# FFN inputs of twelve passes: transposed in 32x32 blocks and copied between partitions instead of on the matmul engine

## The chip, the cores and the metric

The kernel runs on one core of a Trainium2 chip. A core has a matmul engine (TensorE, PE in the profile), a vector engine (VectorE, DVE), a scalar engine for activations and copies (ScalarE, ACT), a general one (GpSimd, POOL) and a sync engine (SyncE, SP) that issues transfers. They run side by side, each in the order of its own instructions, and wait for each other through semaphores. SBUF is the on-chip memory with 128 partitions; PSUM is where TensorE puts its results. The metric is the device time of one execution in microseconds (us).

## The reference

A batch of 2048 tokens x (512 values each) goes through two residual layers.

- First layer: the layer norm of x goes through one of four experts, chosen by the token's id. An expert has one matrix M (its transpose is `ctxT`), used for all three products: `y = (silu(h M^T) * (h M^T)) M^T`. Then `x = x + tanh(g_xattn) * y`.
- Second layer: the layer norm of the new x goes through a feed-forward network, `h = silu(silu(xr w1^T) w3^T) w2^T`, and a router picks the two largest of eight logits `xr wr^T` for each token. The gated rows are added up by expert number with `out.at[indices].add(...)`, so only the first eight rows of the flat output receive anything, the sums over all tokens. They are multiplied by `tanh(g_ffn)`.

Everything is 32-bit floating point.

## The kernel before

**Passes.** The tokens are sorted by expert and cut into 17 passes of 128 rows: 13 full passes (numbers 0 to 12, one expert each) and four shared ones (13 to 16), in which four groups of 32 rows have each their own expert. A full pass needs one 1 MB matrix, a shared pass four. `order` (line 383) says in which place each pass is worked: here the shared passes stand in places 6, 10, 13 and 16.

**A round.** The loop over `i` (line 876) works on several passes at once. Its program order, which is each engine's order (the schedule is written by hand), is:

- `up(order[i])`: TensorE computes z, ScalarE and VectorE make g from it (lines 466, 467);
- `turn_in(order[i+1])`: TensorE transposes the next pass's normalized input (tp_a), ScalarE copies it to SBUF as hT;
- `centre(order[i+2])`: VectorE's statistics and subtraction on the pass after that;
- `gather(order[i+3])` on GpSimd's queue and `load(order[i+3])` of its matrices on SyncE's queue, into seven buffers (`mp`);
- `down(order[i-1])`: TensorE computes y, VectorE adds it to x (line 481), GpSimd scatters the rows to the output;
- `turn_out(order[i-2])`: TensorE transposes the second norm's output h_f with four 128x128 transposes (tp_f, line 380), and ScalarE copies the result into hT2, the FFN's input (line 515; for a shared pass in four pieces at computed places, line 527);
- `norms(order[i+2], order[i-1])`: VectorE's statistics of the new x, two inverse roots of nine small operations each (lines 355 to 373), and h_f = (x - mean) * rs (line 505);
- a `step()` of the FFN, if a block runs;
- `turn_mid(order[i])`: TensorE transposes g (tp_g);
- another `step()`.

**The FFN.** It works on two blocks of 1024 tokens. `sums_of_hT` (line 591) starts a block: TensorE computes the router's logits for both halves (`lg`, tag x, a PSUM pool of two buffers), VectorE subtracts two quarters of the input (T1), turns the logits in 32x32 blocks (`lt`, line 710) and makes T2 to T4. `first_layer` computes the 2x2 block product with seven products (X, Y and Z; the T and S sums feed them), where X takes the tag x too. It yields after every second product, seven times for a block. `second_layer` computes v, four tiles for each half, one a step, and `acc` adds the gated rows up. A block has 15 steps (block 1 ends with some longer ones). Block 0 starts in the round of place 10, with no step at that round's end; block 1 starts when the last pass has been turned out.

**Queues.** SyncE issues the matrices, the weights (w1 and wr in the round of place 2, w3 and w2 in that of place 7) and the final rows, in program order, and waits for a buffer to come free before an issue. GpSimd issues gathers and scatters.

The line that lets block 0 start without a step, and the allocation of the logits:

```python
            if last[b] == i - 2:
                hT_sums[b] = sums_of_hT(b)
                running.append(ffn(b))
        if last[0] != i - 2:
            step()
...
        lg = ps_x.tile([P, P], F32, tag="x", name=f"lg_{b}_{half}")
...
            xs_[c] = ps_x.tile([P, HB], F32, tag="x", name=f"X_{b}_{c}")
```

Of the kernel before, what the change touches and what calls it, by code (L numbers as in the profile page):

```python
# [25 lines left out]
def tile_gated_moe_ffn(  # L26
# [39 lines left out]

    nc = tc.nc
# [17 lines left out]
    mp = ctx.enter_context(tc.tile_pool(name="mp", bufs=7))  # L85
    xp = ctx.enter_context(tc.tile_pool(name="xp", bufs=5))
# [26 lines left out]
    def load_w(src, name):  # L113
        w = ct_([P, KC, src.shape[1]], F32, name)
        nc.sync.dma_start(w, src.rearrange("(k p) f -> p k f", p=P))
        return w
# [188 lines left out]
    def row_tables():  # L305

        pad = ct_([P, NP], F32, "pad")
        nc.vector.tensor_scalar(pad, tok, 1.0, float(4 * NT), ALU.is_lt, ALU.mult)
        nc.vector.scalar_tensor_tensor(to_row, tok, -1.0, pad, ALU.add, ALU.add)

        pads = ct_([P, E], F32, "pads")
        nc.vector.tensor_sub(pads, size[:, 2, :], num[:, 0, :])
        behind = ct_([P, E, NU - NF], F32, "behind")
        nc.vector.tensor_tensor(
            behind,
            later[:, E : 2 * E, NF:NU],
            pads.unsqueeze(2).to_broadcast([P, E, NU - NF]),
            ALU.mult,
        )
        psum = ct_([P, NU - NF], F32, "psum")  # L320
        nc.vector.tensor_reduce(psum, behind.rearrange("p e n -> p n e"), AX.X, ALU.add)
        nc.vector.tensor_sub(psum, place0[:, NF:NU], psum)
        nc.vector.tensor_scalar(
            first, psum, float(-(NB - 1) * TB), float(TB), ALU.add, ALU.min
        )


    hT2 = [ct_([P, KC, TB + (Q if b == NB - 1 else 0)], F32, f"hT2_{b}") for b in range(NB)]
# [9 lines left out]
    def moments(xt, name):  # L338
        st = small.tile([P, 6], F32, tag="st", name=f"st_{name}")
        nc.vector.bn_stats(st, xt)  # L340
        mv = small.tile([P, 2], F32, tag="mv", name=f"mv_{name}")
        nc.vector.bn_aggr(mv, st)
        return mv

    def inverse_roots(mvs_, names):


        n = range(len(names))

        def new(tag):  # L350
            return [small.tile([P, 1], F32, tag=tag, name=f"{tag}_{name}") for name in names]

        v, r, q, w, rs = new("v"), new("r"), new("q"), new("w"), new("rs")
        for i in n:
            nc.vector.tensor_scalar_add(v[i], mvs_[i][:, 1:2], EPS)
        for i in n:
            nc.vector.tensor_scalar(
                r[i].bitcast(I32), v[i].bitcast(I32), -0.5, float(0x5F3759DF), ALU.mult, ALU.add
            )
        for i in n:  # L360
            nc.vector.scalar_tensor_tensor(q[i], r[i], v[i], r[i], ALU.mult, ALU.mult)
        for i in n:
            nc.vector.tensor_scalar(w[i], q[i], 0.375, -1.25, ALU.mult, ALU.add)
        for i in n:
            nc.vector.tensor_scalar(w[i], w[i], q[i], 1.875, ALU.mult, ALU.add)
        for i in n:
            nc.vector.tensor_mul(r[i], r[i], w[i])
        for i in n:
            nc.vector.scalar_tensor_tensor(q[i], r[i], v[i], r[i], ALU.mult, ALU.mult)
        for i in n:  # L370
            nc.vector.tensor_scalar(q[i], q[i], -0.5, 1.5, ALU.mult, ALU.add)
        for i in n:
            nc.vector.tensor_mul(rs[i], r[i], q[i])
        return rs
# [8 lines left out]
    order = [0, 1, 2, 3, 4, 5, NF, 6, 7, 8, NF + 1, 9, 10, NF + 2, 11, 12, NF + 3]  # L383
    assert sorted(order) == list(range(NP))
    xs, x1s, mvs, rss, hs, hTs, gTs, gs, hs2, mats = {}, {}, {}, {}, {}, {}, {}, {}, {}, {}

# [9 lines left out]

    def centre(p):

        mvs[p] = moments(xs[p], f"a{p}")
        hs[p] = work.tile([P, D], F32, tag="h", bufs=4, name=f"h_a{p}")  # L400
        nc.vector.tensor_scalar(hs[p], xs[p], mvs[p][:, 0:1], None, ALU.subtract)  # L401

    def scale(*ps):
        for p, rs in zip(ps, inverse_roots([mvs.pop(p) for p in ps], [f"a{p}" for p in ps])):
            rss[p] = rs
# [6 lines left out]
    def first_in(p):  # L412

        st = small.tile([P, 6], F32, tag="st", name=f"st_a{p}")
        nc.vector.bn_stats(st, xs[p])
        mvs[p] = small.tile([P, 2], F32, tag="mv", name=f"mv_a{p}")
        nc.vector.bn_aggr(mvs[p], st)
        hTs[p] = work.tile([P, KC * P], F32, tag="hT", bufs=2, name=f"hT_{p}")
        n = D // 2
        for i in range(2):  # L420
            h = work.tile([P, n], F32, tag="h", bufs=4, name=f"h_a{p}_{i}")
            nc.vector.tensor_scalar(
                h, xs[p][:, i * n : (i + 1) * n], mvs[p][:, 0:1], None, ALU.subtract
            )
            tp = ps_tp.tile([P, n], F32, tag="tp", name=f"tp_a{p}_{i}")
            for k in range(n // P):
                nc.tensor.transpose(tp[:, k * P : (k + 1) * P], h[:, k * P : (k + 1) * P], ident)
            nc.scalar.copy(hTs[p][:, i * n : (i + 1) * n], tp)  # L428

    def load(p):  # L430

        n0, n = (p, 1) if p < NF else (NF + (p - NF) * G, G)
        mats[p] = []
        for i in range(n0, n0 + n):
            at = nc.values_load(
                look_up(i),
                engines=[SP],
                min_val=0,
                max_val=(E - 1) * D,
                skip_runtime_bounds_check_because="an expert's number, times D",  # L440
            )
            m = mp.tile([P, KC, D], F32, tag="m", name=f"m_{i}")
            nc.sync.dma_start(m, ctxT[bass.ds(at, D), :].rearrange("(k p) f -> p k f", p=P))
            mats[p].append(m)
# [47 lines left out]
    def norms(p_in, p_out):  # L492


        if p_out is None:
            return
        xt = x1s.pop(p_out)
        mv = [moments(xt, f"f{p_out}")]
        names = [f"f{p_out}"]
        if p_in is not None:  # L500
            mv.append(mvs.pop(p_in))
            names.append(f"a{p_in}")
        rs = inverse_roots(mv, names)
        h = work.tile([P, D], F32, tag="h", bufs=4, name=f"h_f{p_out}")
        nc.vector.tensor_scalar(h, xt, mv[0][:, 0:1], rs[0], ALU.subtract, ALU.mult)
        hs2[p_out] = h
        if p_in is not None:
            rss[p_in] = rs[-1]

    def turn_out(p):  # L510

        tp = transposed(hs2.pop(p), f"f{p}").rearrange("p (k t) -> p k t", k=KC)
        if p < NF:
            b, t = divmod(p, TB // P)
            nc.scalar.copy(hT2[b][:, :, t * P : (t + 1) * P], tp)  # L515
            return
        for i in range(G):
            n = (p - NF) * G + i
            place = NF * P + n * Q - (NB - 1) * TB
# [3 lines left out]
                min_val=min(place - E * (Q - 1), TB),  # L523
                max_val=min(place, TB),
                skip_runtime_bounds_check_because="its place less at most E (Q - 1) pads, at most TB",
            )
            nc.scalar.copy(hT2[NB - 1][:, :, bass.ds(at, Q)], tp[:, :, i * Q : (i + 1) * Q])
# [47 lines left out]
    def sums_of_w1():  # L575

        h = D // 2
        a11, a12 = w1[:, 0:2, 0:h], w1[:, 2:4, 0:h]
        a21, a22 = w1[:, 0:2, h:D], w1[:, 2:4, h:D]
        ss = [ffp.tile([P, 2, h], F32, tag=f"S{i}", name=f"S{i}") for i in range(1, 5)]  # L580
# [10 lines left out]
    def sums_of_hT(b):  # L591
# [3 lines left out]
        b11, b12 = hT2[b][:, 0:2, 0:HB], hT2[b][:, 0:2, HB:TB]  # L595
        b21, b22 = hT2[b][:, 2:4, 0:HB], hT2[b][:, 2:4, HB:TB]
        ts = [ffp.tile([P, 2, HB], F32, tag=f"T{i}", name=f"T{i}_{b}") for i in range(1, 5)]
# [7 lines left out]
    def first_layer(b):  # L605
# [14 lines left out]
        def product(out_ps, a, bb, c, start):  # L620
            for k in range(2):
# [3 lines left out]
                    bb[:, k, :],  # L625
# [66 lines left out]
    def logits(b, half):  # L692
# [3 lines left out]
        for k in range(KC):  # L696
            cols = hT2[b][:, k, half * HB : (half + 1) * HB].rearrange("p (t c) -> p t c", t=TT)
# [127 lines left out]
    last = {b: max(i for i, p in enumerate(order) if min(p // (TB // P), NB - 1) == b) for b in range(NB)}  # L825
# [20 lines left out]
    load(order[0])  # L846
# [3 lines left out]
    load(order[1])  # L850
# [8 lines left out]
    load(order[2])  # L859
    nc.sync.dma_start(gates[:, 0:1], g_xattn.to_broadcast([P, 1]))  # L860
    nc.sync.dma_start(gates[:, 1:2], g_ffn.to_broadcast([P, 1]))
    load(order[3])
# [10 lines left out]
    load(order[4])  # L873
    summing = sums_of_w1()
    owed = []
    for i in range(2, NP + 2):
        if i < NP:
            up(order[i])
        if i + 1 < NP:
            turn_in(order[i + 1])  # L880
        if i + 2 < NP:
            centre(order[i + 2])
        if i + 3 < NP:
            gather(order[i + 3])
            load(order[i + 3])
        if i <= NP:
            down(order[i - 1])
        turn_out(order[i - 2])
        if i <= NP:
            norms(order[i + 2] if i + 2 < NP else None, order[i - 1])  # L890
        step()
        if i > NP:
            step()
        if 5 <= i < 9:
            next(summing)
        if i == 2:
            w1 = load_w(w1T, "w1")
            wr = load_w(wrT, "wr")
        if i == 7:
            w3 = load_w(w3T, "w3")  # L900
            w2 = load_w(w2T, "w2")
        if i < NP:
            turn_mid(order[i])
        for b in range(NB):
            if last[b] == i - 2:
                hT_sums[b] = sums_of_hT(b)
                running.append(ffn(b))
        if last[0] != i - 2:
# [54 lines left out]
```

## Time and profile before

| what | value |
|---|---|
| time, median of 3 runs | 279.15 us (279.06 to 279.7) |
| profiled execution | 277.53 us, its span 275.8 us |
| PE, DVE, ACT, POOL busy | 97%, 54%, 25%, 14% |
| granted TensorE clock | 1.0 throughout |
| tp_f transposes | 68, 17 passes of four |
| h_f on VectorE (line 505) | 17 of 542 ns |
| x after y on VectorE (line 481) | 17 of 749 ns |
| statistics of the new x (line 340) | 17 of 695 ns |
| transposes of the logits (line 710) | 4 of 303 ns |
| SyncE's issue of a matrix | 372 ns at the least, 2479 ns at the most |
| moved by DMA | 42.54 MB, mean 154 GB/s |

In a row of groups the columns are the line, the engine, the operation, its output and inputs by name, their shape and how many there are; after the bar the busy time in us and the mean of one in ns; after the second bar the idle time just before them and what ended it. A row of the order of time has the start in us, the duration in us, the engine, the line, the operation, its names and how many were merged; in brackets stands the idle time before it. Starts and ends of matmuls in the order of time are modelled and overlap by some tenths; the chain that ended last merges the same work without overlaps.

### The profile page before, as it was taken

The page shows a single profiled execution, that of the slowest core. Times are in us where ns is not written, and L with a number is a line of the kernel's source. Part 1 is how long each engine was busy: PE and PEld are TensorE (multiplying, and loading weights), DVE is VectorE, ACT ScalarE, POOL GpSimd, SP SyncE. Part 2 cuts the span into 40 slices and gives each one's busy share as a digit, 9 for nine tenths or more (in the row PEclk, how much of TensorE's full clock was granted, in tenths as well). Part 3 has the DMA queues.
Part 4 walks back from the last instruction along what each step waited for, and adds up shares of the span by engine and source line. Part 5 has one row for each costly group of instructions (what it writes and reads, how often), then busy time and mean ns, then how long its engine had stood idle before and what let it go on. Part 6 is the DMA issues. An engine that isn't in the chain of part 4 may idle for free.

```text
span 275.8 us, 3562 instructions
## 1 busy us (share of the span) xinstructions
PE 266.6 (97%) x1173; PEld 125.4 (45%) x1173; DVE 148.7 (54%) x593; ACT 69.3 (25%) x134; POOL 39.3 (14%) x63
## 2 busy tenths in 40 slices
PE   5889999999999999999999999999999999999994
PEld 2445455544355454444344444534245444344362
DVE  6677877777888769918263481516253620711000
ACT  2022232232232231223143232312113233311120
POOL 6520122221122211211110010101010000000000
PEclk9999999999999999999999999999999999999999
DMA  0697998545669996697304084001000000000000
GB/s 1 217 354 277 408 402 334 173 155 206 228 225 402 389 409 258 173 398 264 112 26 166 2 312 180 38 0 40 0 12 2 0 0 1 0 0 2 0 0 2
DMA packets 20722, 42.54 MB, mean 154 GB/s; under 512 B 2143, under 2 KB 2207, under 8 KB 20704
## 3 DMA queue, kind: packets, MB, share of 16 engines
q1 hardware_dynamic: 17952, 33.66, 34.0%
q0 software_dynamic: 2720, 8.65, 8.3%
q8 instruction: 9, 0.15, 0.2%
q14 instruction: 9, 0.07, 0.1%
q10 hardware_dynamic: 32, 0.01, 0.0%
HBM read 38.10 MB, written 4.47 MB: 154 GB/s over the span
## 4 chain that ended last, share of the span: by engine, by line
PE 94%; DVE 2%; DMA 2%; issue 1%; ACT 0%; DVEq 0%
PE z L453 22%; PE y L453 21%; PE v L730 20%; PE X L622 10%; PE Y L622 5%; PE tp_f L380 3%; PE tp_a L380 3%; PE tp_g L380 3%; PE Z L622 2%; PE acc L742 1%; PE lg L699 1%; DMA x<-in_x_dram,from_row 1%; DMA idt<-in_ids_dram 1%; PE accT L758 1%; PE o L814 0%
## 5 line engine op out<-in xcount | busy, mean ns | idle before, releaser
L453 PE MATMUL z<-m,hT 128*32 128x512 f32 (+1 forms) x232 | 61.8, 595 | 0.2 <-ACT hT L428 0.2
L453 PE MATMUL y<-m,gT 128*32 128x512 f32 (+1 forms) x232 | 61.4, 594 | 0.0
L730 PE MATMUL v<-w,s 128*128 128x512 f32 (+1 forms) x136 | 57.3, 570 | 0.0
L730 PEld LDWEIGHTS v<-w,s 128*128 128x128 f32 x136 | 25.0, 190 | 27.2 <-issue 26.7
L453 PEld LDWEIGHTS z<-m,hT 128*32 128x32 f32 (+1 forms) x232 | 22.6, 146 | 29.5 <-issue 28.1
L453 PEld LDWEIGHTS y<-m,gT 128*32 128x32 f32 (+1 forms) x232 | 22.6, 146 | 27.8 <-issue 27.8
L482 POOL DMA_INDIRECT out_dram<-x,to_row x17 | 17.2, 1011 | 84.9 <-DVE x L481 82.7
L389 POOL DMA_INDIRECT x<-in_x_dram,from_row x17 | 16.7, 984 | 77.5 <-DVE h_a L401 22.9
L467 DVE SCALAR_TENSOR_TENSOR g<-z,rs_a,g 128x512 f32<-128x512 f32 x17 | 12.7, 750 | 27.1 <-ACT g L466 27.0
L466 ACT ACTIVATE g<-z,rs_a 128x512 f32<-128x512 f32 x17 | 11.7, 687 | 51.3 <-PE z L453 51.3
L481 DVE SCALAR_TENSOR_TENSOR x<-y,tg,x 128x512 f32<-128x512 f32 x17 | 12.7, 749 | 16.9 <-PE y L453 16.8
L738 ACT ACTIVATE s<-v 128x512 f32<-128x512 f32 (+1 forms) x17 | 9.7, 572 | 41.9 <-PE v L730 41.9
L515 ACT COPY hT<-tp_f 128x512 f32<-128x512 f32 x13 | 7.6, 587 | 43.5 <-PE tp_f L380 43.5
L340 DVE BATCH_NORM_STATS2 st_a<-x 128x6 f32<-128x512 f32 x16 | 11.0, 688 | 7.5 <-DMA x<-in_x_dram,from_row 7.5
L622 PE MATMUL X<-T,S 128*128 128x512 f32 x32 | 15.0, 592 | 0.0
L380 PEld LDWEIGHTS tp_f<-ident,h_f 128*128 128x128 f32 x68 | 8.2, 141 | 10.2 <-issue 10.2
L340 DVE BATCH_NORM_STATS2 st_f<-x 128x6 f32<-128x512 f32 x17 | 11.8, 695 | 0.6
L380 PEld LDWEIGHTS tp_a<-ident,h_a 128*128 128x128 f32 x64 | 7.7, 140 | 9.4 <-issue 9.1
L640 DVE TENSOR_TENSOR s<-X,c 128x512 f32<-128x512 f32 x4 | 2.8, 692 | 16.2 <-PE X L622 16.2
L473 ACT COPY gT<-tp_g 128x512 f32<-128x512 f32 x17 | 10.0, 586 | 5.3 <-PE tp_g L380 5.3
L380 PE MATMUL tp_f<-ident,h_f 128*128 128x128 f32 x68 | 10.4, 276 | 0.0
L380 PE MATMUL tp_g<-ident,g 128*128 128x128 f32 x68 | 10.2, 273 | 0.0
(165 smaller groups left out, 271.6 us busy)
## 6 DMA issues: line engine op xcount, KB each, us to landing
m<-in_ctxT_dram SPq DMA_DIRECT2D x29, 1024.0 KB
w<-in_w1T_dram SPq DMA_DIRECT2D x1, 1024.0 KB
w<-in_w3T_dram SPq DMA_DIRECT2D x1, 1024.0 KB
w<-in_w2T_dram SPq DMA_DIRECT2D x1, 1024.0 KB
x<-in_x_dram,from_row POOLq DMA_INDIRECT x17, 6.2
out_dram<-x,to_row POOLq DMA_INDIRECT x17, 6.1
wr<-in_wrT_dram SPq DMA_DIRECT2D x1, 64.0 KB
x_first<-out_dram SPq DMA_DIRECT2D x4, 4.0 KB
```

The source lines that it names most:

```text
L340: nc.vector.bn_stats(st, xt)
L380: nc.tensor.transpose(tp[:, k * P : (k + 1) * P], h[:, k * P : (k + 1) * P], ident)
L389: nc.gpsimd.indirect_dma_start(out=xt, out_offset=None, in_=x, in_offset=bass.IndirectOffsetOnAxis(ap=from_row[:, p : p + 1], axis=0),)
L453: nc.tensor.matmul(out_ps[i * n : (i + 1) * n, :], lhs[:, k * P + i * n : k * P + (i + 1) * n], m[:, k, :], start=(k == 0), stop=(k == KC ...
L466: nc.scalar.activation(g, z, AF.Silu, scale=rs)
L467: nc.vector.scalar_tensor_tensor(g, z, rs, g, ALU.mult, ALU.mult)
L473: nc.scalar.copy(gT, tp)
L481: nc.vector.scalar_tensor_tensor(xt, y, tg[:, 0:1], xt, ALU.mult, ALU.add)
L482: nc.gpsimd.indirect_dma_start(out=out, out_offset=bass.IndirectOffsetOnAxis(ap=to_row[:, p : p + 1], axis=0), in_=xt, in_offset=None, bou ...
L622: nc.tensor.matmul(out_ps, a[:, k, c * P : (c + 1) * P], bb[:, k, :], start=start and k == 0, stop=k == 1, skip_group_check=True,)
L730: nc.tensor.matmul(v, s1[:, k, c_b + t * P : c_b + (t + 1) * P], w3[:, k, c0 : c0 + n], start=(k == 0), stop=(k == KC - 1),)
L738: nc.scalar.activation(s2, v, AF.Silu)
```

## The change

Passes 0 to 11 no longer go through TensorE for the FFN's input.

- `norms` computes for them only the inverse root and a shift (-mean * rs). Both roots, that of the pass going out and that of the pass coming in, are computed together as two columns in 11 operations. `norm_out`, two rounds after the pass's `up`, makes h_f on ScalarE with scale and shift.
- `turn_set` transposes h_f on VectorE in 32x32 blocks, which leaves the blocks in the wrong partitions. Four passes make a set. When a set is complete, `exchange` issues 16 copies on SyncE's queue, each from 32 partitions to 32 partitions within SBUF with 2 KB a partition, which put the blocks of the set's four passes in their places. The turned sets 0 and 1 lie in s1, which the FFN writes later, set 2 in the buffer that w2 takes afterwards.
- hT2 is four tiles of 512 tokens, each one half of a block: three of them are filled by exchanges, the last by `turn_out` as before (passes 12 to 16). The products and logits read a half as four pieces of 128 columns.
- The shared passes move to places 9, 12, 14 and 16.
- Matrices are loaded as soon as the seventh one before has been used (`load_free`), after `down`, instead of three places ahead. w1 and wr move to the round of place 3, w3 to that of place 12 and w2 to that of place 16. The sums of w1 (S) move from the rounds of places 5 to 8 to 6 to 9; the third of them is written over a quarter of w1.
- x gets six buffers instead of five, h three instead of four.
- The first `step()` of a round stands before `norms` instead of behind it. Block 0 starts in the round of place 11, and a step follows at once. The rounds of places 13 and 15 get a third step.

```diff
-    xp = ctx.enter_context(tc.tile_pool(name="xp", bufs=5))
+    xp = ctx.enter_context(tc.tile_pool(name="xp", bufs=6))
...
-    hT2 = [ct_([P, KC, TB + (Q if b == NB - 1 else 0)], F32, f"hT2_{b}") for b in range(NB)]
+    NS = NF // 4 * 4
+    hT2 = [ct_([P, G, KC, P], F32, f"hT2_{b}") for b in range(NB * 2 - 1)]
+    hT2.append(ct_([P, KC, HB + Q], F32, "hT2_last"))
...
+    def inverse_roots(var, name):
+        n = var.shape[1]
...
+        nc.vector.tensor_scalar_add(v, var, EPS)
+        nc.vector.tensor_scalar(
+            r.bitcast(I32), v.bitcast(I32), -0.5, float(0x5F3759DF), ALU.mult, ALU.add
+        )
+        square()
+        nc.vector.tensor_scalar(w, q, 0.375, -1.25, ALU.mult, ALU.add)
+        nc.vector.tensor_mul(w, w, q)
+        nc.vector.scalar_tensor_tensor(r, w, 1.875, r, ALU.add, ALU.mult)
+        square()
+        nc.vector.tensor_scalar(q, q, -0.5, 1.5, ALU.mult, ALU.add)
+        nc.vector.tensor_mul(rs, r, q)
...
-    order = [0, 1, 2, 3, 4, 5, NF, 6, 7, 8, NF + 1, 9, 10, NF + 2, 11, 12, NF + 3]
+    order = [0, 1, 2, 3, 4, 5, 6, 7, 8, NF, 9, 10, NF + 1, 11, NF + 2, 12, NF + 3]
...
+    def load_free(i):
+        n = len(loaded)
+        while n < len(units) and (n < MP or order.index(units[n - MP][0]) < i):
+            n += 1
+        load(n - len(loaded))
...
+        if p_out < NS:
+            shift = small.tile([P, 1], F32, tag="shift", name=f"shift_{p_out}")
+            nc.vector.scalar_tensor_tensor(
+                shift, mv[:, 0, 0:1], -1.0, rs[:, 0:1], ALU.mult, ALU.mult
+            )
+            scaled[p_out] = rs[:, 0:1], shift
+            return
...
+    def norm_out(p):
+        rs, shift = scaled.pop(p)
+        h = work.tile([P, D], F32, tag="h", bufs=3, name=f"h_f{p}")
+        nc.scalar.activation(h, x1s.pop(p), AF.Identity, bias=shift, scale=rs)
+        hs2[p] = h
...
+    def turn_set(p):
+        b, i = divmod(p, 4)
+        nc.vector.transpose(
+            turned_set(b).rearrange("p q (k i t) -> p k q i t", i=4, t=Q)[:, :, :, i, :],
+            hs2.pop(p).rearrange("p (k q t) -> p k q t", k=KC, q=4),
+        )
+
+    def exchange(b):
+        for q in range(4):
+            for g in range(G):
+                nc.sync.dma_start(
+                    hT2[b][q * Q : (q + 1) * Q, g].rearrange("p k c -> p (k c)"),
+                    turned_set(b)[g * Q : (g + 1) * Q, q, :],
+                )
...
+        if before_last < NS:
+            norm_out(before_last)
         if i + 2 < NP:
             centre(order[i + 2])
         if i + 3 < NP:
             gather(order[i + 3])
-            load(order[i + 3])
+        if before_last in (7, 11):
+            turn_set(before_last)
+        if before_last == 7:
+            exchange(1)
         if i <= NP:
             down(order[i - 1])
-        turn_out(order[i - 2])
+        load_free(i)
+        if before_last == 11:
+            exchange(2)
+        if before_last >= NS:
+            turn_out(before_last)
+        step()
         if i <= NP:
             norms(order[i + 2] if i + 2 < NP else None, order[i - 1])
-        step()
         if i > NP:
             step()
-        if 5 <= i < 9:
+        if 6 <= i < 10:
             next(summing)
-        if i == 2:
+        if i == 3:
             w1 = load_w(w1T, "w1")
             wr = load_w(wrT, "wr")
-        if i == 7:
+        if i == 12:
             w3 = load_w(w3T, "w3")
+        if i == 16:
             w2 = load_w(w2T, "w2")
         if i < NP:
             turn_mid(order[i])
-        for b in range(NB):
-            if last[b] == i - 2:
-                hT_sums[b] = sums_of_hT(b)
-                running.append(ffn(b))
-        if last[0] != i - 2:
+        if i == 11:
+            hT_sums[0] = sums_of_hT(0)
+            running.append(ffn(0))
+        if i == NP + 1:
+            hT_sums[1] = sums_of_hT(1)
+            running.append(ffn(1))
+        step()
+        if before_last in hs2:
+            turn_set(before_last)
+            if before_last == 3:
+                exchange(0)
+        if i in (13, 15):
             step()
```

## The prediction

> **What bounds the kernel now.** I read the engines' busy shares first, then the chain of work that ended last, then the groups by line, and last the order of time at the two places where the change alters what TensorE (PE) meets. All times are us.
>
> ```profile
> PE 266.6 (97%) x1173; PEld 125.4 (45%) x1173; DVE 148.7 (54%) x593; ACT 69.3 (25%) x134; POOL 39.3 (14%) x63
> ...
> PE 94%; DVE 2%; DMA 2%; issue 1%; ACT 0%; DVEq 0%
> PE z L453 22%; PE y L453 21%; PE v L730 20%; PE X L622 10%; PE Y L622 5%; PE tp_f L380 3%; PE tp_a L380 3%; PE tp_g L380 3%; PE Z L622 2%; PE acc L742 1%; PE lg L699 1%; DMA x<-in_x_dram,from_row 1%; DMA idt<-in_ids_dram 1%; PE accT L758 1%; PE o L814 0%
> ...
> L515 ACT COPY hT<-tp_f 128x512 f32<-128x512 f32 x13 | 7.6, 587 | 43.5 <-PE tp_f L380 43.5
> ...
> L380 PE MATMUL tp_f<-ident,h_f 128*128 128x128 f32 x68 | 10.4, 276 | 0.0
> ```
>
> PE is the bound from the first product to the last: the chain is 94% PE, and its pieces follow each other without a gap from 24 on. So every us that leaves PE leaves the time, unless PE has to wait where it did not. tp_f, the transposes of the FFN's inputs, is 3% of the chain. Its mean of 276 ns includes pipelining; the place it really takes is in the order of time.
>
> The order of time where FFN block 0 begins (pass in place 10):
>
> ```profile
> 101.34 0.60 PE L380 MATMUL tp_f<-ident,h_f 128*128 128x128 f32 x4
> 101.78 0.60 PE L380 MATMUL tp_g<-ident,g 128*128 128x128 f32 x4
> 101.79 0.74 DVE L481 SCALAR_TENSOR_TENSOR x<-y,tg,x 128x512 f32<-128x512 f32 x1
> 102.31 1.95 PE L699 MATMUL lg<-hT,wr 128*32 128x128 f32 x64
> 102.56 0.69 DVE L340 BATCH_NORM_STATS2 st_f<-x 128x6 f32<-128x512 f32 x1
> 104.19 3.70 PE L453 MATMUL z<-m,hT 128*128 128x512 f32 x8
> 105.43 0.54 DVE L505 TENSOR_SCALAR h_f<-x,mv_f,rs_f 128x512 f32<-128x512 f32 x1
> 105.89 1.22 DVE L598 TENSOR_TENSOR T<-hT 128x1024 f32<-128x1024 f32 x1
> 107.03 0.50 DVE L710 STREAM_TRANSPOSE lt<-lg 128x128 f32<-128x128 f32 x2
> ```
>
> Four tp_f take 0.44 of PE (101.34 to 101.78). VectorE (DVE) turns the router's logits (lt) only at 107.03, long after PE made them; PE has the next z to do meanwhile.
>
> And where block 1 begins:
>
> ```profile
> 207.24 0.60 PE L380 MATMUL tp_f<-ident,h_f 128*128 128x128 f32 x4
> 207.68 3.60 PE L730 MATMUL v<-w,s 128*128 128x512 f32 x8
> 209.22 0.27 ACT L527 COPY hT<-tp_f 128x128 f32 x1 [0.16 <-ACT hT L527]
> 209.52 1.23 DVE L598 TENSOR_TENSOR T<-hT 128x1024 f32<-128x1024 f32 x1 [5.32 <-ACT hT L527]
> 211.21 1.95 PE L699 MATMUL lg<-hT,wr 128*32 128x128 f32 x64
> 213.09 1.98 PE L622 MATMUL X<-hT,w 128*128 128x512 f32 x4
> ```
>
> Here one step of block 0 (v, 3.44 in the chain) covers ScalarE's (ACT) four copies, which end at 209.49, and T.
>
> **The change, part by part.**
>
> *Transposes gone from PE.* 12 of 17 passes lose four tp_f each: 12 x 0.435 (0.43 and 0.44 at 51.40 and 101.34) = 5.2 saved on the bound. Behind a shared pass's y the chain gives tp_f 0.59; three of the removed ones stand there, and I take it that the next transpose inherits the extra 0.16 (if not, 5.7).
>
> *Their place in the chain.* The ACT copy (587 ns) becomes an Identity with scale and bias; the SBUF-to-SBUF Silu of 629 ns and the one with a scale per row of 687 ns bound it. ACT is 25% busy and it comes behind the two ACT jobs that PE awaits: nothing. On DVE h_f (0.54) goes, 18 small operations of 1.92 together (45.19 to 47.11) become 11 dependent ones and a shift at 0.2 each, the pace of a lone chain (nine from 201.75 to 203.65): 2.4. A 32x32-block transpose of 128x512 comes in; the 128x128 one took 303 ns, a quarter of the elements. 512 columns cost bn_stats 695 ns and four single transposes would cost 1.21; I take 0.7, because other 128x512 operations with one result per input are all near it. DVE's round was 6.29 (stt x 0.77, st_f 0.73, aggregate 0.22, roots 1.92, h_f 0.55, stt g 0.75, st_a 0.72, aggregate 0.22, h_a 0.41); now it is 6.3 + 0.7 = 7.0, and 7.7 in four rounds with a sum of w1 (0.68). PE's round falls from 8.18 to 7.74. g is then ready 1.3 to 2.0 before its transposes: nothing.
>
> *48 copies on SP's queue.* SP spent 0.28 to 0.37 on an issue (L915, L443), so 16 take 4.5 to 6, and 1 MB moves in 2.6 at the 400 GB/s of the busy slices. I put the transpose of set 1 at 90.0 on the new clock, its copies landing by 98 to 100, and the logits that read it at 106.6: covered by 7 to 9. Behind it on SP stands one matrix, needed at 115. Set 0 has nearly 40 in hand, set 2 three rounds; behind set 2 stand only w2 and the small x_first loads.
>
> *Loads by free buffers.* SP waits for y of the seventh matrix before. Tightest are the last two matrices of the passes in places 14 and 16, issued as the shared y two rounds earlier ends. Before, three loads issued at 157.64 had moved two loads' worth by 166.0: 8.4. PE has 10.9 to do by then (three steps of 3.44, a transpose, 0.16): 2.5 in hand, nothing lost. w1 moves behind the matrix that waits for y of place 2 (about 43), and its sums start at 66; w3 is issued some 15 ahead of its use.
>
> *New wait 1, block 0's start.* Before, no step followed the logits of block 0. Now one does, in the round of place 11, and its first product X takes a PSUM buffer (two share the tag x) that the logits hold until DVE has turned them. DVE runs in program order: x, the statistics and roots of that round, T1, then lt. In the chain y ended at 101.51, and the first lt at 107.03 + 0.30 = 107.33: 5.8 later. PE gets from y to X in 0.44 + 0.44 + 1.88 = 2.75. The difference is 3.1; DVE's x will no longer be held 0.25 by h_a (59.75 to 59.78 where it wasn't), and the roots cost 0.1 to 0.2 more than what goes. I take 3.0, between 2.8 and 3.4. Queued behind X on PE is everything.
>
> *New wait 2, block 1's start.* Steps: block 0 has 15; they now begin one earlier and two are added at places 13 and 15, so all are spent a round before the end, where one was left before to stand at 207.68. tp_f ends at 207.84 in the chain; the copies end 1.65 later, T1 2.9, lt 3.25. Half 0's logits (0.94) no longer depend on those copies, half 1's end at 2.65. X starts at 3.25 where 1.88 would be ideal: 1.4, between 1.1 and 1.75 (both halves waiting).
>
> *Sum.* -5.2 + 3.0 + 1.4 = -0.8. The profiled execution took 277.53 (span 275.8 and 1.7 around it), 1.6 under the median of 279.15; I carry the difference over: 279.15 - 0.8 = 278.35.
>
> [...]
>
> **The rivals.**
>
> *Fewer new waits.* Speaking for it: I infer which buffer X takes. Without wait 2 the time is 277.0, without wait 1 275.4, without either 273.9. Against it: both waits are made of measured rows, and PE has nothing else in its order there.
>
> *DVE becomes the bound (slower).* Place: rounds 2 to 10. With 1.21 per transpose and 0.25 per small two-column operation its round is 6.3 + 0.6 + 1.21 = 8.1, over PE's 7.74; it decides from there. Nine rounds of 0.36 and four sums of 0.69 make 6.0; less 2.0 in hand that is 4: 282.4. Halfway, about 0.6: 279.0. Against it: DVE had 1.5 to 2.1 idle in each round.
>
> *Matrices late (slower).* If the four loads of place 13's round land together instead of in order, 8.4 + 2 x 2.75 = 13.9 against 10.9: 3.0 lost, 281.4. It decides when two loads take over 10.9.
>
> *Copies late (slower).* From 1.04 per copy (16.6 between 90.0 and 106.6) the logits wait; 1.3 would cost 4: 282.4. For it: with its queue full, SP took 4.2 for an issue (wr at 24.22). Against it: the queue has one load in it here, and 0.37 is the dearest steady issue.
>
> **How the numbers follow.** The forecast, both waits and no other: 0.42, its own range 277.7 to 278.9. Without wait 2 0.12, without wait 1 0.06, without either 0.04. DVE 0.16, matrices 0.15, copies 0.05. About 0.3% (0.84) is what can be told from no change, so the borders are 278.31 and 279.99. The forecast lies on the lower one: 0.19 faster, 0.23 same. With 0.22 from fewer waits faster is 0.41. Of DVE 0.04 and of the matrices 0.05 stay within the band: same 0.32. The rest of these three is slower, 0.27. The range of 276.6 to 281.4 leaves out 0.10 below (no wait 1) and some 0.08 above.
>
> **What would show it.** 20 instead of 68 tp_f; PE idle of about 3 before the first X, put down to lt, and 1.4 before the X or lg of block 1; a DVE transpose near 0.7, 12 times; no PE wait for m, and none for g before place 11. The forecast is wrong if X of block 0 starts right behind the logits, or if PE waits for g or m.

## The result and the profile after

The changed kernel takes 280.10 us (median of 20 executions, 278.91 to 281.56), the kernel before beside it 279.08 (20 executions, 278.47 to 279.80). The ratio is 1.0045, with a 95% interval of 1.0029 to 1.0061: slower by about 1.2 us. The forecast was 278.35, so 1.75 was missed. The profiled execution has a span of 277.5 instead of 275.8.

From the page of the kernel after: the busy shares, the clock granted to PE, the chain that ended last, and the group of first products with its idle time.

```profile
PE 265.4 (96%) x1125; PEld 121.5 (44%) x1125; DVE 149.8 (54%) x507; ACT 72.0 (26%) x134; POOL 39.3 (14%) x63
...
PEclk9999999999999999799999999999999999999998
...
PE 82%; DVE 6%; DMA 5%; SPq 4%; issue 2%; ACT 0%; ACTq 0%; DVEq 0%
...
L703 PE MATMUL X<-hT,w 128*128 128x512 f32 x16 | 9.4, 720 | 1.9 <-DVE lt L791 1.9
```

There are 48 fewer matmuls, as the change says, and yet PE's busy time falls by 1.2 only. The chain is no longer nearly all PE: DVE, DMA and SP's issues (SPq) have shares of 4 to 6%. (Its way to DMA and SP hangs on one wait of T, 0.21 at 110.07 in the rows below, put down to a matrix that T does not read, so no more is built on it here.) PE waits 1.9 for the turned logits, and not for any matrix. One slice of the clock row shows a 7: PE did not run at full speed there. And the 16 X products take 720 ns each, where the 16 Z products of the same shape take 592.

The order of time around block 0's start (place 11 now):

```profile
89.97 10.86 SPq L583 DMA_DIRECT2D hT<-s  x16
94.06 3.64 PE L488 MATMUL y<-m,gT 128*32 128x512 f32 x32
101.83 8.87 SPq L470 DMA_DIRECT2D m<-in_ctxT_dram  x6
102.00 3.60 PE L488 MATMUL y<-m,gT 128*128 128x512 f32 x8
105.44 0.60 PE L394 MATMUL tp_f<-ident,h_f 128*128 128x128 f32 x4
106.40 1.96 PE L780 MATMUL lg<-hT,wr 128*32 128x128 f32 x47
108.70 0.43 PE L780 MATMUL lg<-hT,wr 128*32 128x128 f32 x3 [0.33 <-issue]
109.45 0.67 PE L780 MATMUL lg<-hT,wr 128*32 128x128 f32 x14 [0.33 <-issue]
110.07 1.23 DVE L679 TENSOR_TENSOR T<-hT,hT 128x1024 f32<-128x1024 f32 x1 [0.21 <-DMA m<-in_ctxT_dram]
111.21 0.51 DVE L791 STREAM_TRANSPOSE lt<-lg 128x128 f32<-128x128 f32 x2
111.58 3.68 PE L703 MATMUL X<-hT,w 128*128 128x512 f32 x4 [1.45 <-DVE lt L791]
115.09 1.88 PE L703 MATMUL Z<-hT,w 128*128 128x512 f32 x4
116.90 3.68 PE L488 MATMUL z<-m,hT 128*32 128x512 f32 x32
```

X starts at 111.58, behind lt, within 0.2 of the forecast's place: tp_f starts 4.1 later than in the kernel before, so y ends at about 105.6, and 2.75 + 3.0 behind it is 111.4. But the first X takes 3.68, against 1.99 of the same product in block 1 below, so z of the pass in place 12 starts at 116.90 instead of about 115.2. This 1.7 is the largest part of what this execution misses: its span of 277.5 is 2.5 over 275.8 - 0.8. The second thing to see is on SP: the 16 copies of set 1 keep it for 10.9, and the matrices behind them are issued from 101.83 on. The y that frees the buffers of three of the four matrices of place 12 is over at 97.7, and the one for the first already at 90.

The granted clock of the kernel after, by stretches (columns: the stretch; the sum; busy time of PE, PEld, DVE, ACT and POOL, each with its count; granted clock; share of the DMA engines; GB/s):

```profile
104.00:108.00 4.00, 3.93 (x57) 2.60 (x56) 3.17 (x9) 1.44 (x5) 1.03 (x2) 1.00 1.04 400
108.00:111.00 3.00, 1.46 (x20) 0.69 (x20) 2.48 (x11) 0.11 (x1) 0.97 (x1) 1.00 1.03 391
111.00:112.00 1.00, 0.42 (x1) 0.43 (x2) 1.00 (x4) 0.00 (x0) 0.00 (x0) 0.81 1.05 420
112.00:115.00 3.00, 3.00 (x4) 1.08 (x4) 3.00 (x3) 0.00 (x0) 0.00 (x0) 0.50 1.04 401
```

PE is idle 2.2 of the 8.0 from 104 to 112, nearly all of it between 108 and 111.6, in pieces of up to 1.45. Then the clock is at half for some 3.4. The DMA engines are full all the while.

Block 1's start in the kernel after:

```profile
210.96 0.60 PE L394 MATMUL tp_f<-ident,h_f 128*128 128x128 f32 x4
212.39 1.93 PE L780 MATMUL lg<-hT_last,wr 128*32 128x128 f32 x32
213.23 1.23 DVE L679 TENSOR_TENSOR T<-hT_last,hT 128x1024 f32<-128x1024 f32 x1 [5.37 <-ACT hT_last L604]
214.38 0.51 DVE L791 STREAM_TRANSPOSE lt<-lg 128x128 f32<-128x128 f32 x2
214.74 1.99 PE L703 MATMUL X<-hT,w 128*128 128x512 f32 x4 [0.42 <-DVE lt L791]
```

From the end of tp_f (211.4 without the overlap) to X it is 3.35; the forecast had 3.25, of which 1.4 is the new wait 2. X stands at 214.74 against 213.09 before: the 1.65 is all of the longer span, so nothing is lost behind it.

### The profile page after: what moved, and what is told of

Its sections match the earlier page's. It is cut to its first block, busy times and chain, and to the rows that moved or that the text cites. A ratio compares the mean times of both kernels' runs of the same rounds, so it can differ in the third digit from the quotient of the medians.

```text
span 277.5 us, 3465 instructions
## 1 busy us (share of the span) xinstructions
PE 265.4 (96%) x1125; PEld 121.5 (44%) x1125; DVE 149.8 (54%) x507; ACT 72.0 (26%) x134; POOL 39.3 (14%) x63
## 4 chain that ended last, share of the span: by engine, by line
PE 82%; DVE 6%; DMA 5%; SPq 4%; issue 2%; ACT 0%; ACTq 0%; DVEq 0%
PE v L811 20%; PE z L488 18%; PE y L488 18%; PE X L703 11%; PE Y L703 5%; SPq L583 4%; DMA m<-in_ctxT_dram 3%; PE Z L703 2%; PE tp_a L394 2%; PE tp_g L394 2%; PE acc L823 1%; DMA x<-in_x_dram,from_row 1%; DVE T L679 1%; PE tp_f L394 1%; DMA idt<-in_ids_dram 1%
## 5 line engine op out<-in xcount | busy, mean ns | idle before, releaser
L502 DVE SCALAR_TENSOR_TENSOR g<-z,rs_f,g 128x512 f32<-128x512 f32 x14 | 10.2, 727 | 23.9 <-ACT g L501 23.9
L501 ACT ACTIVATE g<-z,rs_f 128x512 f32<-128x512 f32 x14 | 9.6, 688 | 42.5 <-PE z L488 36.9
L703 PE MATMUL Y<-T,w 128*128 128x512 f32 x32 | 15.0, 592 | 0.0
L394 PEld LDWEIGHTS tp_g<-ident,g 128*128 128x128 f32 x68 | 8.3, 141 | 9.1 <-issue 9.1
L703 PE MATMUL X<-hT,w 128*128 128x512 f32 x16 | 9.4, 720 | 1.9 <-DVE lt L791 1.9
L356 DVE BATCH_NORM_STATS2 st_a<-x 128x6 f32<-128x512 f32 x16 | 10.9, 683 | 0.3 <-DMA x<-in_x_dram,from_row 0.3
```

The costliest lines, as they stand in the source:

```text
L502: nc.vector.scalar_tensor_tensor(g, z, rs, g, ALU.mult, ALU.mult)
L703: nc.tensor.matmul(out_ps, a[:, k, c * P : (c + 1) * P], bb[:, k], start=start and k == 0, stop=k == 1, skip_group_check=True,)
```

## The experiments

Two theories stood after the first reading. *Clock*: the waits at block 0's start let the clock fall, and this is the whole of the miss. *Matrices*: the copies hold SP, the four matrices of place 12 come late, and z of place 12 could not have started much earlier anyway. Each kernel below is the kernel after with the edit shown, unless it is said otherwise.

**1. Keep PE busy between the logits and X.** Two products that nobody reads are put there.

```diff
             running.append(ffn(0))
+            warm = ps_y.tile([P, HB], F32, tag="y", name="warm")
+            for _ in range(2):
+                nc.tensor.matmul(warm, ident, w1[:, 0, :], start=True, stop=True)
```

> Two 32-bit products of 128x512 (four PE instructions, 1.7 us at full clock) into the free buffer y are put between block 0's logits and its first X; nothing reads them. Theory A (PE's idling at block 0's start halves its clock, and that cost 1.9 us on top of the wait): the granted clock stays at 1.0 there, the four X take 1.7 to 2.0 instead of 3.7, X starts at most 0.3 later, and the time falls by about 1.6, to 278.5. Rival (the clock fell for another reason, or the fill only delays X): the clock is 0.5 there as before and the time is 280.1 to 280.6.

Measured: 280.29 (279.41 to 283.69), ratio to before 1.0046 [1.0024, 1.0067]. The time is that of the kernel after, although the clock in the profiled run stays at 1.00 from 104 to 118. Its order of time:

```profile
111.88 1.88 PE L703 MATMUL X<-hT,w 128*128 128x512 f32 x4
115.40 1.06 PE L488 MATMUL z<-m,hT 128*32 128x512 f32 x6
117.32 3.62 PE L488 MATMUL z<-m,hT 128*32 128x512 f32 x26 [0.86 <-DMA m<-in_ctxT_dram]
```

X takes 1.88 and z starts at 115.40, as theory A had it. Then z waits for the fourth of its matrices, and the time is the rival's. With the gap filled the clock does not fall in this profiled run; in one of the 12 executions, the slowest, the mean clock is 0.991 all the same. So the idling goes with the fall of the clock (8 shows it again), but the clock alone is not the cause of the miss.

**2. Turn the logits earlier on DVE.** In the round of place 11, lt goes ahead of the statistics and roots, and T1 to T4 behind the round's step.

```diff
+        def subtract():
+            nc.vector.tensor_sub(ts[1], b22, ts[0])
+            nc.vector.tensor_sub(ts[2], b22, b12)
+            nc.vector.tensor_sub(ts[3], b21, ts[1])
+
+        if b == 0:
+            lts[b] = [turned(b, half, lg) for half, lg in enumerate(lgs)]
+            late_sums.append(lambda: nc.vector.tensor_sub(ts[0], b12, b11))
+            late_sums.append(subtract)
+            return b11, b21, b22, ts
...
-        if i <= NP:
+        if i <= NP and i != 11:
             norms(order[i + 2] if i + 2 < NP else None, order[i - 1])
...
             running.append(ffn(0))
+            norms(order[i + 2], order[i - 1])
...
         step()
+        while late_sums:
+            late_sums.pop(0)()
```

> In the round of place 11 VectorE turns block 0's logits first, then does that round's norms, then the sum of the first step, then T1 to T4. Theory A (X waits for VectorE): X starts when the logits end, at about 110 or earlier instead of 111.6, the clock stays at 1.0, and the time falls by 1.5 + 1.9 = 3.4, to 276.7. Rival B (the late copies and matrices set the pace): the wait moves, the logits wait for hT2 or z of place 12 waits for its matrices until about 117, and the time falls by less than 1.

Measured: 281.0 (280.03 to 283.16), ratio 1.0076 [1.0045, 1.0107]. Its order of time:

```profile
109.91 1.98 PE L711 MATMUL X<-hT,w 128*128 128x512 f32 x4
113.54 1.05 PE L488 MATMUL z<-m,hT 128*32 128x512 f32 x4
116.14 1.05 PE L488 MATMUL z<-m,hT 128*32 128x512 f32 x2 [1.55 <-DMA m<-in_ctxT_dram]
118.62 3.62 PE L488 MATMUL z<-m,hT 128*32 128x512 f32 x26 [1.43 <-DMA m<-in_ctxT_dram]
```

The new wait 1 is gone: X follows the logits and z begins 3.4 earlier than in the kernel after. All of it is lost again at the next place, 3.0 of it as a wait for m. z takes the four matrices in turn, so these are the waits for the third and the fourth: they land at about 116 and 118.6, although PE was there earlier.

**3. Undo the new wait 2.** One step is kept back, so that one is left to cover block 1's start.

```diff
-        step()
+        if i != 16:
+            step()
```

> The first step of the round of place 16 is left out, so that block 0's last step remains for the round that starts block 1, where it covers ScalarE's copies and T1. Theory A: wait 2 goes (X of block 1 follows the logits at once), the time falls by 1.4, to 278.7. Rival: the step is missed in the round of place 16, where PE then waits for g or its matrices, and the time stays at 280.1.

Measured: 279.32 (277.88 to 280.79), ratio 0.9998 [0.9976, 1.0020]. That is 0.8 less than the kernel after by the medians and 1.3 less by the ratios (1.0045), where 1.4 was priced; the interval is too wide to tell these apart. X of block 1 follows the logits at once, and the profiled run again waits for m, 1.24 at 117.9. With edit 2 as well:

> Both of the last two edits. Theory A: the gains add, 280.1 - 3.4 - 1.4 = 275.3, under the kernel before by 3.8. Rival B: at most 1 + 1.4, 277.7.

Measured: 278.90 (277.74 to 282.80), ratio 0.9996 [0.9975, 1.0017]. z of place 12 begins at 113.76 and waits 2.4 for m. Taking both waits away brings 1.2 together by the medians, 1.4 by the ratios, where theory A had 4.8: the rest is held by the matrices.

**4. The wait and the clock without the rest of the change.** The kernel before, with a step right behind block 0's logits.

```diff
-        if last[0] != i - 2:
-            step()
+        step()
```

> The kernel before with one edit: block 0 takes a step in the round in which it starts, as the changed kernel does. All transposes stay on TensorE, no copies within SBUF. Theory A: all of the loss appears here without the rest of the change: X waits 3.1 for the turned logits, the clock falls to 0.5 for 3.4 us (1.9), and block 1's start has no step left to cover it (1.4 to 1.7): 279.1 + 6.4 to 6.7 = 285.6. If an idle PE doesn't halve the clock by itself: 283.7. Rival B (the loss is from the copies and the new order of loads): 279 to 280.

Measured: 284.63 (283.94 to 285.55), ratio 1.0188 [1.0158, 1.0217]. Its order of time:

```profile
108.03 3.23 PE L622 MATMUL X<-hT,w 128*128 128x512 f32 x4 [1.53 <-DVE lt L710]
111.05 2.37 PE L622 MATMUL Z<-hT,w 128*128 128x512 f32 x4
```

The step at once costs some 5.3 here, with no exchange and the old order of passes. X waits 1.53 for lt after the same gaps in the logits, and X and Z run at a granted clock of 0.81 and then 0.50: together 5.6 of modelled time instead of 3.9. Theory A had 285.6, rival B 280 at the most. So wait and clock belong to the place of the first step, not to the copies.

**5. Only the transposes go back to PE.** The 12 passes are transposed by PE, in the new order of passes; the 32x32 transposes and the copies are gone.

```diff
-        nc.vector.transpose(
-            turned_set(b).rearrange("p q (k i t) -> p k q i t", i=4, t=Q)[:, :, :, i, :],
-            hs2.pop(p).rearrange("p (k q t) -> p k q t", k=KC, q=4),
+        tp = transposed(hs2.pop(p), f"f{p}")
+        nc.scalar.copy(
+            hT2[b][:, :, :, i * Q : (i + 1) * Q],
+            tp.rearrange("p (k g t) -> p g k t", k=KC, g=G),
         )
...
         if before_last >= NS:
             turn_out(before_last)
+        else:
+            turn_set(before_last)
```

> The changed kernel with the twelve passes' transposes back on TensorE (four 128x128 transposes and a ScalarE copy into the same layout of hT2), without VectorE's transposes and the 48 copies; order, loads, roots and steps stay as changed. Theory A: 12 x 0.435 come back on PE, the two waits and the halved clock stay: 280.1 + 5.2 = 285.3. Rival B (the copies delay the matrices and the logits): less than that, 282 to 284, since what the copies cost goes with them.

Measured: 282.16 (281.69 to 283.02), ratio 1.0115 [1.0083, 1.0147]. It is 2.1 slower than the kernel after, not 5.2; this is rival B's range. The clock is 1.000 in all four executions, X waits 1.15 for lt, and the matrices are in time:

```profile
114.85 1.98 PE L697 MATMUL X<-hT,w 128*128 128x512 f32 x4 [1.15 <-DVE lt L785]
118.48 3.64 PE L488 MATMUL z<-m,hT 128*32 128x512 f32 x32
```

So what is left of the change costs 3.1 against the kernel before, and the blocks on DVE with their copies bring 2.1 of the 5.2 that PE no longer does.

**6. A quarter of the copies.** Set 1 is exchanged with 4 copies instead of 16. Three quarters of that tile are zero: the inputs are missing there, and the kernel computes the rest as before.

```diff
-        for q in range(4):
+        for q in range(1 if b == 1 else 4):
...
+        if i == 5:
+            nc.gpsimd.memset(hT2[1], 0.0)
```

> The changed kernel with 4 instead of 16 copies for set 1 (three quarters of the second tile of hT2 keep zeros that GpSimd writes earlier, so those inputs are missing from the FFN). SyncE is then free about 7.5 earlier, and the matrices of place 12 are issued when y of place 9 ends, near 97.7 instead of 101.8. Theory D (two limits meet at z of place 12, near 117: PE's own wait for the turned logits with the halved clock, and the matrices held up behind the copies; either alone keeps it there): z stays at 116.5 to 117, the time at 280. Rival E (the copies alone are the loss): z starts about 113.5 and the time falls by 3, to 277.

Measured: 278.14 (277.27 to 279.64), ratio 0.9977 [0.9954, 1.0000]. This lies between theory D's 280 and rival E's 277. SP issues the four copies in 2.4 and the matrices from 93.98 on; z of place 12 has no wait for m, and the profiled run has the slow X:

```profile
112.26 3.38 PE L703 MATMUL X<-hT,w 128*128 128x512 f32 x4 [1.49 <-DVE lt L791]
117.58 3.64 PE L488 MATMUL z<-m,hT 128*32 128x512 f32 x32
```

The 12 executions fall into two groups: seven with a mean granted clock of 0.996 to 0.998 take 277.27 to 278.28, five with 0.990 to 0.992 take 278.95 to 279.64. Once the matrices are in time, the lower clock is seen in the time, at about 1.5. Edit 2 on top of it:

> The same with the logits turned first, as in the run that did only that. Theory D: with both limits gone z of place 12 starts near 113.5 instead of 117 to 118.6, and the time is 276.5 to 277. Rival A (only PE's wait and the clock count, and the matrices come when they come): z still waits for its matrices until 117 or later, 280 or more.

Measured: 275.63 (275.22 to 276.50), ratio 0.9882 [0.9853, 0.9912]. Edit 2, worth nothing alone, is worth 2.5 here, and the time is 0.9 under theory D's range.

**7. All the copies, half of them on GpSimd's queue.** Nothing is left out.

```diff
-                nc.sync.dma_start(
+                (nc.gpsimd if b == 1 and q >= 2 else nc.sync).dma_start(
```

> The changed kernel, complete, with half of set 1's 16 copies issued on GpSimd's queue instead of SyncE's. Theory D: as with few copies, the matrices come earlier but PE's own wait holds z of place 12 at 117: 280. Rival E: 277 to 278. GpSimd's scatters may come late by some us, which nothing waits for.

Measured: 279.21 (278.40 to 281.88), ratio 1.0017 [0.9991, 1.0043]. Its order of time:

```profile
89.77 5.77 SPq L583 DMA_DIRECT2D hT<-s  x8
90.03 4.05 POOL L583 DMA_DIRECT2D hT<-s  x8 [4.54 <-DVE s L575]
96.56 26.92 SPq L470 DMA_DIRECT2D m<-in_ctxT_dram  x7
111.79 1.98 PE L703 MATMUL X<-hT,w 128*128 128x512 f32 x4 [1.62 <-DVE lt L791]
115.42 2.78 PE L488 MATMUL z<-m,hT 128*32 128x512 f32 x24
```

Again the time lies between D's 280 and E's 277 to 278. SP is free 5.3 earlier, and z of place 12 starts at 115.42 with no wait, at the 115 that the prediction gave it. From 104 to 108 and from 108 to 110 the full DMA engines carry 412 and 403 GB/s, against 400 and 385 in the kernel after; what moved is SP's 10.9 of issuing, now 5.8.

**8. Both remedies, and the split again beside it.** The split of 7 with the two products of 1; and the kernel of 7 once more on the same chip.

> The kernel after with both remedies that were so far tried alone: half of set 1's copies on GpSimd's queue, so that the matrices of place 12 are there in time, and two products that no one reads on PE between block 0's logits and X, so that the granted clock does not fall. Nothing of the computation is left out. Theory (two limits meet at z of place 12, and the clock is what still parts the split kernel's executions into about 278.8 and 280.5): every execution is of the quicker kind, mean granted clock 0.996 or more, median 278.4 to 278.9, X of block 0 at about 111.8 in 2.0, z at about 115.4 without a wait for m. Rival (the two kinds of execution have another cause than the idling at block 0's start): executions at a clock of 0.985 to 0.991 stay as frequent as with the split alone (5 of 12), median 279.2 as there.

> The same kernel as the split one, beside the one with the two products on one chip: median 279.2, executions at a clock of 0.985 to 0.991 again some 4 in 10, and these 1.5 above the others.

Measured: 278.73 (278.38 to 279.00), ratio 0.9988 [0.9970, 1.0006], clock 0.994 to 1.000 in all six executions; and 280.22 (278.12 to 280.38), ratio 1.0023 [0.9995, 1.0051], clock 0.988 to 0.990 in four executions and 0.994 and 0.996 in two. First the split with the products, then the split alone, each in its order of time:

```profile
110.25 1.98 PE L1000 MATMUL warm<-w,ident 128*128 128x512 f32 x4
112.08 1.88 PE L703 MATMUL X<-hT,w 128*128 128x512 f32 x4
115.60 3.64 PE L488 MATMUL z<-m,hT 128*32 128x512 f32 x32
```

```profile
111.84 3.54 PE L703 MATMUL X<-hT,w 128*128 128x512 f32 x4 [1.46 <-DVE lt L791]
115.18 2.06 PE L703 MATMUL Z<-hT,w 128*128 128x512 f32 x4
117.17 1.07 PE L488 MATMUL z<-m,hT 128*32 128x512 f32 x8
```

The split with the products came as its theory had it. The split alone came out at 280.22 instead of 279.2, because four of its six executions were of the slower kind. Its profiled one has the halved clock (0.50 from 113 to 115), the one shown under 7 has not; it is the same kernel. Over both runs of the split alone, nine executions with a clock up to 0.991 have a median of 280.24, nine from 0.994 on 278.79: the halved clock costs 1.45. None of the six executions with PE kept busy is of the slower kind. (The mean clock is a rough sign: it also holds a fall at the end of the span, and the profiled run of 3 has 0.994 with the fall at block 0 in it. The times part the two kinds more clearly.)

**9. A version that beats both.** The split of 7 with edits 2 and 3, complete.

> Complete, with all three edits: half of set 1's copies on GpSimd's queue, block 0's logits turned before the norms, and one step left for block 1's start. Theory D: z of place 12 near 114 and no wait at block 1's start: 280.1 - 3 - 1.4 = 275.7, under the kernel before by 3.4. If GpSimd's copies take long, the logits wait for them and the time is 278 to 279.

Measured: 275.73 (275.37 to 277.19), ratio 0.9902 [0.9868, 0.9935]: at theory D's 275.7, and by the ratio 2.7 less than the kernel before, by the medians 3.5 (279.21 beside it). Its order of time:

```profile
110.49 1.99 PE L711 MATMUL X<-hT,w 128*128 128x512 f32 x4
114.12 3.64 PE L488 MATMUL z<-m,hT 128*32 128x512 f32 x32
```

No wait for lt, none for m, and a clock of 1.00 from 106 to 126.

## Why the prediction was wrong

**What failed first: the copies on SP's queue.** The step "SP spent 0.28 to 0.37 on an issue (L915, L443), so 16 take 4.5 to 6" was taken from rows of another shape. A copy from 32 partitions to 32 of 2 KB each takes SP 0.59 by the median of 32, and 10.9 for 16 with what lies between them. The range from 0.28 to 0.37 did not hold it, and the rival of late copies looked at the wrong reader: it asked when the logits would wait (from 1.04 on), not when the queue behind would. "Behind it on SP stands one matrix, needed at 115" is the sentence that broke. The first matrix of place 12 did stand there, but by the time SP was free, three more of that pass and the next pass's were due as well. The DMA engines, with hardly more than copies to move, had carried 58 to 221 GB/s in the stretches from 90 to 100, against 357 to 421 in the kernel before (two rows of the kernel after, then two of the one before; the last figure is GB/s):

```profile
90.00:92.00 2.00, 2.00 (x8) 1.04 (x7) 1.86 (x5) 0.59 (x1) 1.02 (x1) 1.00 0.24 58
98.00:100.00 2.00, 2.00 (x8) 1.04 (x7) 1.86 (x5) 0.59 (x1) 1.02 (x1) 1.00 0.42 100
```

```profile
90.00:92.00 2.00, 2.00 (x6) 0.82 (x5) 0.68 (x1) 0.37 (x1) 0.00 (x0) 1.00 1.02 357
98.00:100.00 2.00, 2.00 (x6) 0.86 (x5) 0.75 (x1) 0.71 (x2) 0.00 (x0) 1.00 1.06 421
```

From 104 to 112 they were full, with a share of 1.03 to 1.05 and 385 to 412 GB/s, and the last two of the four matrices landed between 116 and 119 (1 to 3). That is the mechanism of the rival of late matrices (loads that land together), at place 12 and not at places 14 and 16, where nothing was lost.

**What failed as well: wait 1 was priced as idle time alone.** Its 3.0 was right, the place of X too, within 0.2; in the trace only 1.45 of it is idle time behind lt, and the rest lies in logits that take 3.7 instead of 1.95. But with the idling the clock can fall for the work behind it, 1.45 by the split's two groups, 1.7 in the profiled run. The sum put nothing for this: it went by the clock of 1.0 of a kernel in which PE had no such gap, and with such a gap the kernel before had the fall too (4).

**Why neither is seen alone.** Both act on z of place 12, and leave it at nearly the same time: it ends at 120.6 by the halved clock in one run (the kernel after), at 120.9 by the matrices in the other (1). The later one sets the time, so taking the clock's fall or the wait away alone brought nothing (1, 2), taking the late matrices away alone brought 279.21 (7), and taking both 278.73 (8), 0.4 over the forecast, of which 0.3 is the added products (X at 112.08 instead of 111.79). In the 20 executions of the kernel after the mean clock separates nothing: six with a clock under 0.992 have a median of 279.6, the other 14 of 280.3. This would fit matrices that are the limit in most of them; only one was profiled, and in it z had no wait for m.

**What held.** The waits: X behind lt at block 0, 3.35 after tp_f at block 1. The work taken from PE: with it back (5) X of block 1 stands at 217.50, without it and without the two limits (8) at 213.40; of the 4.1 between them 0.3 are the added products and about 0.5 the shorter wait for lt, so 4.4 to 4.9 stand against the 5.2; the rest is a small miss of its own. The 32x32 transpose takes 0.70, as taken; the Identity on ACT takes 0.82, over its bound of 0.69, with one wait of 0.4 for it on DVE and none on PE; DVE was no bound, since no g is waited for. Places 14 and 16 had their matrices.

The rivals of fewer waits and of DVE as the bound fell. With the two limits gone the kernel with the transposes on DVE takes 278.73 (8), with PE doing them in the new order 282.16 (5). Against the kernel before, 278.73 is no gain that the interval shows; the time of 9 is. SP issued the 16 copies of set 1 in 10.9, and in the trace their 512 packets are through by about 102, 12 after the first issue and before the logits of 106.4.

**What stays open.** In every kernel profiled in which block 0's step follows its logits at once (with or without the two products between), the 64 logits take 3.5 to 4.0 instead of 1.95, with gaps of 0.2 to 0.45 that the profile puts down to no engine; in the kernel before they have none, nor has block 1 of the kernel after. In 2 and 9, where X follows the logits at once, they cost some 1.7. No run was made on their cause. They are no work of the copies, since 4 and 5 have them too. Nor is it settled how much of the 1.4 leaving the step of 3 brought.

## What to carry to other kernels

Price a transfer's issue by a row of its own shape, and ask what stands behind it in its queue when the burst is long, not only who reads its result. A wait on the bound engine can have a second price: in five traces here the clock fell to 0.50 around the X before which PE had idled for 2.1 to 2.3 us of 3.6 to 4.3, and in a sixth, with 2.4 of 3.8, it stayed at 1.00. So either fill the gap with work or move the work that it waits for. When two limits meet at one instruction, undoing each alone can show nothing; undo both before a theory is given up.

## What was not expected of the hardware

- In the kernel after the clock fell to 0.50 for about 3.4 after 2.1 of idle time within 3.6 (108.0 to 111.6), none of its pieces over 1.5. In 3, 4, 6 and the second split of 8 it fell too, after 2.2 to 2.3 of idle time in the 3.8 to 4.3 up to X. In the split shown under 7 PE is idle for 2.4 in the 3.8 up to X, and the clock stays at 1.00; it is the same kernel as the second split, and of its 18 executions nine have a mean clock up to 0.991. Nor did 1.9 in the 4.9 up to X bring a fall in 5, or 2.4 in the 4.0 from 114 to 118, without logits in it, in 2. So the length of the idle time alone does not tell whether the clock falls. No run shows what else counts.
- One copy of 64 KB between partitions in SBUF takes SP 0.59 to issue, GpSimd 0.51 (8 in 4.05), while the kernel before issued 1 MB in 0.37 at the least.
